# A two-layer graph network: the last projection in float32r passes instead of block sums in fp32

## The chip, the cores and the metric

The kernel runs on one core of one Trainium2 chip. The metric is the device time of one execution in microseconds (us), taken as the median of several runs.

## The reference

Two graph attention layers follow one another on a batch of 64 graphs of 256 nodes with 512 features, each with its own adjacency matrix. Every layer is preceded by a layer norm and a relu, and its result is added to its input. What is computed, cut to what matters:

```python
h = jnp.maximum(_layernorm(x), 0.0)
x = x + L0(adj, h)          # two GAT stages
h = jnp.maximum(_layernorm(x), 0.0)
x = x + L1(h, adj)

# L0: gat(h, W1: 512 -> 4 heads x 256), elu, gat(., W2: 1024 -> 512, one head)
xl = (x @ W).reshape(B, N, H, F)
e = leaky_relu(asrc[:, :, None, :] + adst[:, None, :, :], 0.2)   # asrc, adst: xl times two vectors
attn = softmax(where(mask, e, -1e9), axis=1)
out = einsum('bsdh,bshf->bdhf', attn, xl) + bias

# L1: W_proj: 512 -> 8 heads x 64
xp = einsum('bnd,do->bno', x, W_proj)
scores = leaky_relu(a_src[:, :, :, None] + a_dst[:, :, None, :] + b_att, 0.2)
att = softmax(where(A > 0, scores, -1e30), axis=-1)
out = relu(einsum('bhij,bhjk->bhik', att, xh))
```

All inputs are float32 (the adjacency is int32), and so is the output.

## The kernel before

The work of one graph is a chain of some 80 small steps. Each step is a method of the class `Graph` (one object for each graph). Steps that end in 1 belong to the first GAT stage (four heads), in 2 to the second, in 3 to the last layer (eight heads).

A stage runs like this. `stats` and `norm` make the layer norm of 256 rows (two blocks t = 0, 1 of 128 rows). `away` and `home` write the result to DRAM and read it back in another arrangement, after which `back` turns 128x512 numbers with VectorE's block transpose, so that the features lie across the partitions. `left` makes sums of blocks on GpSimd. The projection follows as a `Product`: the matrix product is cut into 2x2 blocks and done with 7 instead of 8 block products, by the Winograd scheme. Each block product is one of p1 to p7 (TensorE, 128 rows of a chunk against 256 columns and a few logit columns, 2 chunks for a 512-feature input, 4 for 1024 features). The steps q1, q6 and q7 copy running sums to SBUF (tile `kept`, ScalarE, line 61), and q2, q3, c22 and q4 put the four blocks of the result in place (line 261 on VectorE, 259 on ScalarE). The right operand's block sums are made once, at the start (`right`, line 592). `m1a` and `m1b` are the two halves of the first projection, `m2` the second, and `m3` the last one: its weights are `wp_sb`, whose first 8 columns hold the logit vectors folded into W_proj, and `put3` writes the logits to `lg3` and the rest to `xl3`.

Then `exp` makes exponentials of the logits on ScalarE, `ship` and `rows` send them through DRAM to all partitions, `edges` forms the attention weights (one ScalarE and one VectorE instruction for each block, lines 291 and 292), `gat` multiplies them with the projected features (lines 411, 481, 556) and `out` divides by the sum that a column of ones has collected. `again` loads x once more into `x2`, `bias` adds b2 to it (line 370, GpSimd), `out2` adds the second stage, and `store` writes the graph's result. `elu1`, `ez1`, `send2`, `take2` stand between the first and the second stage. `masks`, `caps`, `open`, `cap3` and `edge01` prepare the adjacency.

The order of all steps is written out by hand in three strings: `head` for the start, `order` for one round, and `tail` for the end. A round advances several graphs at once: "-3 m3 q4" is a step of the graph three places behind the newest one. The string `order` runs 61 times, for r = 2 to 62. Each engine executes its own instructions strictly in the sequence of the strings, and a step waits only for its inputs and for a free buffer. All DMAs shown here but a few at the start are issued from SP's queue, in the sequence of the strings too.

Buffers come from pools with a fixed number for each name: `x2` 3, `hs` (the turned input of m1 and m3) 2, `e` 9, `kept` 4, `o` 4, and in PSUM 2 banks of `sum`, 4 of `pm`. The last graph (`gone` false) turns its data on TensorE with identity products (lines 228, 453) and spreads its logits with identity products too (line 254).

After `short_path` a second path for inputs of extreme range stands in the program; it is entered only when the range check asks for it.

## Time and profile before

| | us |
|---|---|
| median of 3 runs | 2969.62 (2968.97 to 2975.85) |
| the profiled execution, its time | 2968.22 |
| its span in the profile | 2966.4 |
| TensorE busy (PE) | 2917.8 |
| VectorE busy (DVE) | 2531.3 |
| ScalarE busy (ACT) | 1711.3 |
| GpSimd busy (POOL) | 1287.4 |

The profile is of one execution. Matrix products overlap in the pipeline, so the mean duration of one is longer than the distance between two starts; the distance is what counts in a full stream. In the groups, a line gives the source line, the engine, the operation, the tile written and the tiles read, the shape and the count, then the busy time in us and the mean duration in ns, and at last the idle time of the engine just before, with what ended it. PEld is the weight load of TensorE, which runs beside PE.

### The profile page before, as it was taken

How to read it: one execution, taken by the hardware profiler on the slowest of the kernel's cores; microseconds unless marked ns; L12 is line 12 of the kernel's file. 1: busy time of each engine (PE TensorE's matmuls, PEld its weight loads, DVE VectorE, ACT ScalarE, POOL GpSimd, SP SyncE). 2: the span in 40 equal slices, each digit the busy share in tenths (PEclk: the TensorE clock that was granted, in tenths of full speed). 3: DMA queues.
4: the chain of work that ended last, by engine and by line, in shares of the span. 5: the costliest groups of instructions: out<-in, count | busy, mean ns of one | idle time of the engine just before them, and what ended most of it. 6: DMA issues, size and time to landing. Idle time of an engine off the chain costs nothing.

```text
span 2966.4 us, 59522 instructions
## 1 busy us (share of the span) xinstructions
PE 2917.8 (98%) x20296; PEld 2531.6 (85%) x20296; DVE 2531.3 (85%) x6370; ACT 1711.3 (58%) x4489; POOL 1287.4 (43%) x1882
## 2 busy tenths in 40 slices
PE   6999999999999999999999999999999999999997
PEld 4888888888888888888888888888888888888886
DVE  8788888888888888888888888888888888888886
ACT  3466565655655655655656556556556556555554
POOL 3443443444444444434444444444444344344433
PEclk9999999999999999999999999999999999999998
DMA  6556555656565665555556565565555556566542
GB/s 193 155 173 180 175 180 171 180 178 179 170 182 176 175 180 174 172 180 177 179 171 185 173 179 173 178 184 167 175 177 174 178 178 179 172 182 176 179 136 73
DMA packets 536859, 513.17 MB, mean 173 GB/s; under 512 B 85736, under 2 KB 373352, under 8 KB 536552
## 3 DMA queue, kind: packets, MB, share of 16 engines
q1 hardware_dynamic: 535176, 507.20, 57.5%
q8 instruction: 165, 2.70, 0.4%
q10 hardware_dynamic: 1376, 2.10, 0.2%
q14 instruction: 142, 1.16, 0.1%
HBM read 332.01 MB, written 168.79 MB: 169 GB/s over the span
## 4 chain that ended last, share of the span: by engine, by line
PE 97%; DVE 1%; DMA 1%; issue 0%; ACT 0%; POOL 0%; SPq 0%; ACTq 0%; DVEq 0%
PE sum L55 38%; PE pm L55 29%; PE pm L411 15%; PE pm L556 8%; PE pm L481 7%; DVE prod L597 0%; DMA w1a_sb<-in_L_gnn_W_dram 0%; DMA xs<-in_x_dram 0%; DMA h<-kept_h 0%; DMA z<-kept_z 0%; DVE e L292 0%; DVE hs L213 0%; ACT h L199 0%; DVE z L419 0%; DMA bc<-kept 0%
## 5 line engine op out<-in xcount | busy, mean ns | idle before, releaser
L291 ACT ACTIVATE wys<-bc,exs_sb 128x256 f32<-128x256 f32 x1646 | 715.4, 468 | 297.4 <-DMA bc<-kept 145.4
L61 ACT ACTIVATE kept<-sum 128x260 f32<-128x260 f32 (+3 forms) x768 | 296.0, 386 | 714.0 <-PE sum L55 713.3
L292 DVE SCALAR_TENSOR_TENSOR e<-wys,exs_sb,cap 128x256 f32<-128x256 f32 x1024 | 444.9, 476 | 62.2 <-ACT wys L291 52.6
L55 PE MATMUL sum<-w_sb,h1s 128*128 128x257 f32 x2048 | 488.1, 380 | 0.6
L411 PE MATMUL pm<-xl,e 128*128 128x257 f32 x2048 | 476.4, 380 | 0.9 <-DVE e L292 0.8
L411 PEld LDWEIGHTS pm<-xl,e 128*128 128x128 f32 x2048 | 387.9, 190 | 60.1 <-DVE e L292 1.7
L55 PEld LDWEIGHTS sum<-w_sb,h1s 128*128 128x128 f32 x2048 | 383.3, 190 | 64.3 <-issue 3.8
L566 POOL TENSOR_TENSOR x<-x,o 128x256 f32<-128x256 f32 x256 | 182.0, 731 | 486.5 <-DVE o L564 484.6
L261 DVE TENSOR_TENSOR xl<-pm,kept 128x256 f32<-128x256 f32 (+2 forms) x768 | 318.1, 415 | 79.1 <-ACT kept L61 40.4
L219 POOL TENSOR_TENSOR hs<-hs 128x256 f32<-128x256 f32 x128 | 109.0, 852 | 617.9 <-DVE hs L213 589.8
L55 PE MATMUL pm<-w_sb,h1s 128*128 128x257 f32 x1536 | 361.6, 384 | 0.0
L55 PEld LDWEIGHTS pm<-w_sb,h1s 128*128 128x128 f32 x1536 | 285.8, 189 | 44.8 <-POOL h1s L219 1.0
L213 DVE STREAM_TRANSPOSE hs<-h 128x512 f32<-128x512 f32 x252 | 283.2, 1150 | 8.4 <-DMA h<-kept_h 8.0
L292 DVE SCALAR_TENSOR_TENSOR e<-wys,exs_sb,mask 128x256 f32<-128x256 f32 x640 | 278.4, 477 | 12.9 <-ACT wys L291 7.0
L449 DVE STREAM_TRANSPOSE h1s<-z 128x512 f32<-128x512 f32 x252 | 260.6, 1104 | 17.6 <-DMA z<-kept_z 17.6
L55 PE MATMUL sum<-w1a_sb,hs 128*128 128x260 f32 x1024 | 269.1, 386 | 4.0 <-DVE w1a_sb L597 3.4
L55 PE MATMUL sum<-wp_sb,hs 128*128 128x264 f32 x1024 | 271.0, 387 | 0.7 <-ACT hs L229 0.7
L55 PE MATMUL sum<-w1b_sb,hs 128*128 128x256 f32 x1024 | 266.4, 383 | 4.9 <-DVE r L417 2.6
L556 PEld LDWEIGHTS pm<-xl,e 128*64 128x64 f32 x8192 | 245.9, 138 | 24.8 <-issue 24.1
L419 DVE SCALAR_TENSOR_TENSOR z<-pm,r,b_sb 128x256 f32<-128x256 f32 x512 | 247.7, 484 | 18.3 <-DVE r L417 0.3
L219 POOL TENSOR_TENSOR h1s<-h1s 128x512 f32<-128x512 f32 x64 | 81.3, 1270 | 412.2 <-DVE h1s L449 405.2
L556 PE MATMUL pm<-xl,e 128*64 128x65 f32 x8192 | 255.8, 223 | 1.9 <-DVE e L292 1.7
(94 smaller groups left out, 4832.0 us busy)
## 6 DMA issues: line engine op xcount, KB each, us to landing
bc<-kept SPq DMA_DIRECT2D x380, 256.0 KB, 4.6
kept_h<-h SPq DMA_DIRECT2D x126, 512.0 KB, 3.5
h<-kept_h SPq DMA_DIRECT2D x126, 512.0 KB, 3.7
kept_z<-z SPq DMA_DIRECT2D x252, 256.0 KB
z<-kept_z SPq DMA_DIRECT2D x252, 256.0 KB, 2.9
xs<-in_x_dram SPq DMA_DIRECT2D x64, 512.0 KB, 6.0
x<-in_x_dram SPq DMA_DIRECT2D x64, 512.0 KB
out_dram<-x SPq DMA_DIRECT2D x64, 512.0 KB
```

The costliest lines, as they stand in the source:

```text
L55: self.nc.tensor.matmul(to[:, :self.n], self.lhs[:, i, c, :], self.rhs[:, i, c, :], start=(first and c == 0), stop=(last and c == self.nk ...
L61: self.nc.scalar.activation(s[:, :self.n], self.sum[:, :self.n], AF.Copy)
L213: nc.vector.transpose(a[:, 4 * t:4 * t + 2].rearrange("p r k (j q) -> p q (r k) j", q=4), h[:, t].rearrange("p (q i c) -> p q c i", q=4, c=4))
L219: nc.gpsimd.tensor_tensor(s1, s3, a22, ALU.add)
L261: nc.vector.tensor_tensor(dst, pm, add, ALU.add)
L291: nc.scalar.activation(wy, bc, AF.Copy, scale=yw)
L292: nc.vector.scalar_tensor_tensor(dst, wy, xw, mask, ALU.max, op)
L411: nc.tensor.matmul(pm[:, :Q + 1], self.e[1, h][:, s, t * P:(t + 1) * P], xl1[:, s, h, L1:], start=(s == 0), stop=(s == T - 1))
L419: nc.vector.scalar_tensor_tensor(self.zt[t][:, sl], pm[:, :Q], r, b1_sb[:, sl], ALU.mult, ALU.add)
L449: nc.vector.transpose(a.rearrange("p k (j q) -> p q k j", q=4), z.rearrange("p (q i c) -> p q c i", q=4, c=4))
L481: nc.tensor.matmul(pm[:, :n], self.e[2][:, s, t * P:(t + 1) * P], xl2[:, s, half, L2:L2 + n], start=(s == 0), stop=(s == T - 1))
L556: nc.tensor.matmul(pv[q:q + 64, h, :], self.e[3, a * G + h][:, s, t * P + q:t * P + q + 64], xl3[:, s, a * G + h, :], start=(s == 0), stop ...
```

## The change

The last projection is no longer a `Product`. Each operand is split into a high and a low part in the type float32r. The weights are split once, at the start: `high` (ScalarE, the raw weights times 1 - 2^-13), `low` (VectorE, the rest), `rest` (VectorE, high minus 2^12 times low) and `lift` (ScalarE, low times 2^12). For each graph and each block of 128 rows, `high3` (ScalarE), `low3` (GpSimd) and `mix3` (VectorE) make three parts of the turned input. For each of the 4 quarters of the result (2 row blocks, 2 column halves) there are three passes of 4 chunks each on TensorE: `u3` (high with high) and `w3` (low with lifted low) into one `sum` bank, and `v3` (mix with rest) into a `pm` bank. `k3` copies the sum times 1 + 2^-12 to SBUF on ScalarE, and `d3` subtracts the v3 result on VectorE and writes it to `xl3`. The two logit columns of each head now lie beside the head's 64 columns, in the weights (`raw3`, `wk_sb`) as in `xl3`, so `lg3` and its adds go.

Buffer numbers change: `x2` 2, `hs` 1 (m1 alone), `e` 7, `kept` 3, `o` 2, `ad` 1, and the norm's small tiles 3; `raw` with 1 and `hk` with 5 buffers are new. The raw projection weights lie in the buffer `h1s` at first.

All three strings are written anew. The diff, with the strings cut to the seam of a round:

```diff
-            self.a1 = work.tile([P, 7, DC // 2, P], F32, name="hs")
+            self.a1 = work.tile([P, 7, DC // 2, P], F32, name="hs", bufs=1)
...
-            self.x2 = work.tile([P, T, D], F32, name="x2", bufs=3)
+            self.x2 = work.tile([P, T, D], F32, name="x2", bufs=2)
...
         def back3(self, t):
-            if self.a3 == 1:
-                self.a3 = work.tile([P, 7, DC // 2, P], F32, name="hs")
-                self.m3 = Product(nc, ps_sum, ps_mm, work, self.a3, wp_sb, put3)
-            (back if self.gone else turn)(self.h, self.a3, t)
-
-        def left3(self):
-            left(self.a3, DC // 2)
+            self.raw = work.tile([P, DC, P], F32, name="raw", bufs=1)
+            (back if self.gone else turn)(self.h, self.raw, t)
+
+        def part(self, i, t):
+            a = self.hk[i, t] = work.tile([P, DC, P], F32R, name="hk", bufs=5)
+            return a
+
+        def high3(self, t):
+            nc.scalar.activation(self.part(0, t), self.raw, AF.Copy, scale=DOWN)
+
+        def low3(self, t):
+            nc.gpsimd.tensor_tensor(self.part(1, t), self.raw, self.hk[0, t].bitcast(F32), ALU.subtract)
+
+        def mix3(self, t):
+            nc.vector.scalar_tensor_tensor(self.part(2, t), self.hk[0, t].bitcast(F32), UP, self.raw, ALU.mult, ALU.subtract)
+
+        def uv(self, pm, i, j, half, t, first, last):
+            for c in range(DC):
+                nc.tensor.matmul(pm[:, :G * (K3 + 2)], self.hk[i, t][:, c], wk_sb[:, j, half, c],
+                                 start=(first and c == 0), stop=(last and c == DC - 1))
+
+        def u3(self, half, t):
+            self.us[half, t] = ps_sum.tile([P, 512], F32, name="sum")
+            self.uv(self.us[half, t], 0, 0, half, t, True, False)
+
+        def w3(self, half, t):
+            self.uv(self.us[half, t], 1, 1, half, t, False, True)
+
+        def k3(self, half, t):
+            s = self.ks[half, t] = work.tile([P, 264], F32, name="kept", bufs=KEPT)
+            nc.scalar.activation(s, self.us.pop((half, t))[:, :264], AF.Copy, scale=UP)
+
+        def v3(self, half, t):
+            self.vs[half, t] = ps_mm.tile([P, 512], F32, name="pm")
+            self.uv(self.vs[half, t], 2, 2, half, t, True, True)
+
+        def d3(self, half, t):
+            def heads(s):
+                return s[:, :G * (K3 + 2)].rearrange("p (h k) -> p h k", h=G)
+            nc.vector.tensor_tensor(xl3[:, t, half * G:(half + 1) * G, :K3 + 2], heads(self.ks.pop((half, t))),
+                                    heads(self.vs.pop((half, t))), ALU.subtract)
...
-        def sums3(self, i):
-            if i == 0:
-                self.sums[3] = right(wp_sb)
-            next(self.sums[3])
...
+        def high(self, half):
+            nc.scalar.activation(wk_sb[:, 0, half], raw3[:, half], AF.Copy, scale=DOWN)
+
+        def low(self, half):
+            nc.vector.tensor_tensor(wk_sb[:, 1, half], raw3[:, half], wk_sb[:, 0, half].bitcast(F32), ALU.subtract)
+
+        def rest(self, half):
+            nc.vector.scalar_tensor_tensor(wk_sb[:, 2, half], wk_sb[:, 1, half].bitcast(F32), -LIFT,
+                                           wk_sb[:, 0, half].bitcast(F32), ALU.mult, ALU.add)
+
+        def lift(self, half):
+            nc.scalar.activation(wk_sb[:, 1, half], wk_sb[:, 1, half].bitcast(F32), AF.Copy, scale=LIFT)
...
     order = """
+        -1 elu1 0 0, -1 ez1 0 1, -3 mix3 1, -2 m2 p3, -3 v3 1 0, -2 m2 q3, -2 m2 p2, -3 d3 1 0, -3 u3 0 0,
+        -3 v3 0 0, -3 w3 0 0, -2 bias 1, -3 low3 1, -1 elu1 1 1, -2 bias 0, 0 away1, 1 load, -3 v3 0 1, 0 home1,
+        -1 elu1 0 1, -2 m2 q2, -2 exp2, -2 ship2, -3 u3 1 1, -3 k3 0 0, 1 stats1 0, -3 w3 1 1, -3 v3 1 1,
+        -3 d3 0 0, -3 u3 0 1, -3 w3 0 1, 0 masks, -3 k3 1 1, 1 stats1 1, -1 send2 0 0, -3 k3 0 1, -1 gat1 2 0,
+        -3 d3 1 1, 0 back1 0, -3 d3 0 1, -1 gat1 3 0, -2 rows2, -1 send2 1 1, 0 back1 1, -1 take2 0 0, -3 batt3,
...
+        -3 edges3 6, 0 m1b p3, -1 m2 p6, -3 out3 0 1, -1 m2 q6, 0 edges1 0, -3 gat3 1 0, -3 gat3 1 1, -1 m2 p7,
+        0 gat1 0 1, -3 out3 1 0, -3 out3 1 1, 0 edges1 3, -3 store, -2 back3 0, 0 gat1 0 0, 0 m1b q3, 0 edges1 1,
+        0 out1 0 0, -1 m2 p5, -2 high3 0, 0 gat1 1 0, -2 low3 0, -2 mix3 0, -2 back3 1, -1 m2 q7, 0 out1 1 0,
+        -1 m2 c22, 0 edges1 2, -1 again, 1 edge01, -2 u3 1 0, 1 norm1 1, 0 gat1 1 1, -2 w3 1 0, 1 norm1 0,
+        -2 k3 1 0, 0 out1 1 1, -1 m2 p4, 0 ez1 0 0, 0 gat1 3 1, 0 gat1 2 1, -2 high3 1, 0 out1 0 1, 0 out1 3 1,
+        0 out1 2 1, 0 ez1 1 1, -1 m2 q4, -3 range
```

## The prediction

> **What bounds the kernel now.** I read the busy table, then the three stages of the span, then TensorE's own waits, then the chain of work that ended last.
>
> ```profile
> PE 2917.8 (98%) x20296; PEld 2531.6 (85%) x20296; DVE 2531.3 (85%) x6370; ACT 1711.3 (58%) x4489; POOL 1287.4 (43%) x1882
> PE 97%; DVE 1%; DMA 1%; issue 0%; ACT 0%; POOL 0%; SPq 0%; ACTq 0%; DVEq 0%
> ```
>
> TensorE is 98% busy and carries 97% of the chain. VectorE, at 85%, is the next engine. By stage (columns: stretch, its length, busy time of PE, PEld, DVE, ACT and POOL, then granted clock, DMA share, GB/s):
>
> ```profile
> 0.00:74.00 74.00, 46.25 (x153) 35.00 (x154) 61.60 (x213) 22.55 (x55) 27.74 (x47) 0.95 0.61 193
> 74.00:148.00 74.00, 70.97 (x324) 60.80 (x324) 58.14 (x133) 36.30 (x96) 30.09 (x41) 1.00 0.53 155
> 148.00:2892.00 2744.00, 2742.97 (x19232) 2387.47 (x19231) 2365.78 (x5897) 1618.07 (x4252) 1204.48 (x1758) 1.00 0.59 176
> 2892.00:2966.00 74.00, 57.56 (x592) 48.30 (x590) 45.75 (x130) 34.36 (x89) 25.05 (x37) 0.90 0.21 74
> ```
>
> A graph is 316 TensorE instructions, so the third row is 19232/316 = 60.9 rounds of 45.1 us, in which TensorE idles 1.03 us in all. The waits of TensorE in that stretch are one line:
>
> ```profile
> PE pm L556 <- issue: 0.2, 1, 0.2
> ```
>
> So in a steady round every TensorE time removed shortens the span, as long as nothing else becomes late. VectorE works 2365.78/2744 = 86% of it, 38.9 us of 45.1.
>
> **What the change removes from TensorE.** The old last projection in the timeline (start, duration, what, count):
>
> ```profile
> 1532.42 1.05 PE L55 MATMUL sum<-wp_sb,hs 128*128 128x264 f32 x4
> 1533.31 1.05 PE L55 MATMUL pm<-wp_sb,hs 128*128 128x264 f32 x4
> 1534.20 1.05 PE L55 MATMUL sum<-wp_sb,hs 128*128 128x264 f32 x4
> ```
>
> Starts are 0.89 us apart for four instructions, 222.5 ns each (the 386 ns of the groups contain overlap). Each fp32 product is two such instructions with two weight loads: the row holds four for two products. Seven pairs of products per graph: 7 x 0.89 = 6.23 us.
>
> **What it adds to TensorE.** Each graph has 4 sums (2 row blocks x 2 column halves) of three passes over 4 chunks: 48 products of 264 columns in float32r. The built program holds one weight load and one matmul for each of these, where fp32 has two. No float32r ran before, so it is bounded. Above: the fp32 instruction of the same 264 columns, 222.5 ns, if the type saves only the second instruction. Below: half of it, 111 ns, if the moving operand too is no longer taken in two parts. A weight load of 128 columns has to hide beside so short a matmul; the nearest rows for that are the identity products of 128 columns in the tail:
>
> ```profile
> 2895.62 1.60 PE L453 MATMUL pm<-ident,z 128*128 128x128 f32 x12
> 2897.06 1.25 PE L55 MATMUL sum<-w_sb,h1s 128*128 128x257 f32 x5
> 2944.61 2.50 PE L254 MATMUL pm<-ident,exs_sb 128*128 128x128 f32 x20 [0.56 <-ACT exs_sb L534]
> ```
>
> Twelve take 1.44 us to the next start, 120 ns each. Twenty last 2.50 us; less the last one's 0.275, that is 2.22/19 = 117 ns. So an instruction with a 128-column load can repeat every 117 to 120 ns, and the load is not added to the matmul. I take 115 ns, between the half (111) and these rows: splitting the weights visibly costs fp32 a second load and stream, and the split of the columns should cost the same again. 48 x 0.115 = 5.52 us. Change per graph: 5.52 - 6.23 = -0.71 us (-0.90 at 111 ns, -0.47 at 120, +4.45 at 222.5). Times 64 graphs: **-45.4 us** (-57.6, -30.1, +284.8).
>
> The Trainium skill bears on both ends. FP8 and Floating Point Precision, section TensorE Precision Notes, counts four passes for true FP32 and names a read truncated to the native width as the reduced form; with that form as one pass, a quarter of 445 ns is 111 ns, by which the sum would be -57.6 us, an estimate. Against the change speaks TensorE: Matmul & The Clock Gate, section Weight-path perf modes: the fast weight load is off for FP32 types. Its section LDWEIGHTS (loading the stationary operand) gives columns/1.2 ns, 107 ns for 128; added to 111 ns that makes 218 ns a product and about +271 us, an estimate, which rows L453 and L254 contradict: they hide such a load.
>
> **The other engines.** From the groups by shape (busy, mean ns):
>
> ```profile
> L428 DVE SCALAR_TENSOR_TENSOR z<-ez,z 128x512 f32<-128x512 f32 x256 | 178.2, 696 | 2.9
> L261 DVE TENSOR_TENSOR xl<-pm,kept 128x256 f32<-128x256 f32 x384 | 158.7, 415 | 5.2 <-PE pm L55 4.7 <-PE pm L556 0.5
> L261 DVE TENSOR_TENSOR xl<-pm,kept 128x260 f32<-128x260 f32 x192 | 81.3, 423 | 69.2 <-ACT kept L61 36.4 <-PE pm L55 32.6
> L261 DVE TENSOR_TENSOR lg<-pm,kept 128x8 f32<-128x8 f32 x192 | 29.5, 154 | 3.5 <-ACT kept L61 2.2 <-PE pm L55 1.2
> L423 ACT ACTIVATE ez<-z 128x512 f32<-128x512 f32 x256 | 158.7, 620 | 7.5 <-DVE z L419 7.5
> L370 POOL TENSOR_TENSOR x<-x,b_sb 128x512 f32<-128x512 f32 x128 | 163.6, 1279 | 31.1 <-DMA x<-in_x_dram 30.8
> ```
>
> VectorE gains four d3 (0.423, the 260-column row) and two mix3 (0.696, the 512-column row), 3.08 us, and loses three adds of 256 and three of 8 columns, 1.71 us: +1.37, so 40.3 us of a 44.4 us round, 91%. ScalarE gains two high3 (0.62) and four k3 (0.39), and loses three copies (0.39) and the two of q4 (0.16 and 0.38): +1.09 on 26.6 us. GpSimd swaps left3's four (0.85 and three of 0.73, 3.05 us) for two low3 (1.28): -0.5 us. That these write float32r is not in any row; I take the float32 price, and no gain: low3 at twice its price would still leave GpSimd under 55%. All of it lies beside TensorE's 44.4 us and costs nothing while each result is on time; if that cover goes, VectorE's next 4 us per round would bound.
>
> **Waits that the new order brings.** The tightest I find goes through the round's seam. x2 has two buffers instead of three, so the reload `again` (on SP's queue, with away1, load and home1 behind it) waits until the store of the graph two before has landed. GpSimd's bias 1 waits for that reload, low3 1 is queued behind bias 1, and w3 1 1 on TensorE waits for low3, with three more float32r groups and two gat1 groups behind it. Price of the chain: a store of 512 KB 3.5 (the row of kept_h), reload 6.0 (the row of xs), bias 1.28, low3 1.28: 12.1 us. Cover: TensorE's work in the new order from the last gat3 plus out3's VectorE and GpSimd parts to w3 1 1, some 14.9 us. Slack 2.8 us. Likewise back3 of the second block waits for low3 of the first (one raw buffer), and six parts share five hk buffers, so that low3 1 waits for u3 0 0 to be done with high3's: both have 1 to 2 us before TensorE asks. The sum tiles alternate between two banks; k3 0 0 follows exp2 on ScalarE, which waits for m2's q2 on VectorE, with about 1 us before u3 0 1. I allow 0.08 us a round, +5 us in 61 rounds (bounds 0 and 0.7). The hs, e, ad, o, kept and small buffers that are trimmed have their last readers half a round before the next writer in the order; nothing.
>
> **Ends.** Head: the four sums of wp (0.81 each, 3.2 us on VectorE) go; low and rest on VectorE come, two each of 1056 columns at about the 1.22 us of the 1028-column sums, 4.9 us, and four ScalarE passes. VectorE is busy 61.6 of the first 74 us, so some of the +1.7 shows: +2 us (-4 to +6, as the whole head is reordered). The tail trades left3 for high3, low3, mix3 in series, about equal: 0 (+-4).
>
> **Sum.** Against the profiled execution (2968.2 us; 1.8 us lies outside its span of 2966.4): 2968.2 - 45.4 + 5 + 2 = 2929.8. The median of the three runs is 1.4 us higher: **2931 us**.
>
> **The rivals.**
> Two-part streams: float32r still takes 222.5 ns. For it: only fp32 was seen. Against: half as many instructions for each product and the column split argued above. 2969.6 + 285 = 3254 us, slower. It decides from 130 ns on, where 48 products cost the old 6.23 us. Chance 0.14.
> The seam or VectorE gives the gain back: waits of 0.4 to 1.2 us per round. For it: 2.8 us slack is less than a landing's own spread (3.5 to 6.0), VectorE at 91%. Against: the order before ran 61 rounds at 86% with 1 us idle. From 2969.6 - 45 + 2 + 24 to +73: 2950 to 3000 us; above 0.7 us a round (43/61) it is slower. Chance 0.20, of which 0.05 faster, 0.07 no change, 0.08 slower.
> Weight load shows at 120 ns: 2946 us, still within the main case.
> Main case, 111 to 120 ns and at most 0.3 us of waits: 2912 to 2948 us, chance 0.64; a remainder of 0.02 goes to slower.
>
> Faster by over 0.3% (9 us, about what a measurement here can tell from no change): 0.64 + 0.05 = 0.69; within 0.07; slower 0.08 + 0.14 + 0.02 = 0.24. The range takes the main case and the seam rival and leaves out two-part streams: 2910 to 3000.
>
> **What would show it.** Right: float32r starts about 115 ns apart, four in 0.46 us; PE busy per round down 0.7 us with idle under 0.2 us; VectorE busy near 91%. Wrong: starts at 220 ns; or TensorE idle of 0.5 us and more per round before L541, released by POOL low3, ACT k3 or VectorE; or in the gat1 and gat3 rows released by VectorE's edges.

## The result, and the profile after

The changed kernel takes 2967.93 us (median of 12 runs, 2965.85 to 2970.23) where the kernel before took 2970.35 us beside it (12 runs, 2967.99 to 2975.85). The ratio is 0.999, 95% interval 0.9981 to 0.9999: no change of a size that counts. The forecast was 2931 us. The profiled execution after took 2966.22 us (span 2964.5), the one before 2968.22 (span 2966.4). So 2.0 us came of the 38 us that the sum had promised.

The busy table and the chain of the kernel after:

```profile
PE 2912.1 (98%) x21576; PEld 2571.5 (87%) x21576; DVE 2602.0 (88%) x6370; ACT 1780.8 (60%) x4557; POOL 1265.4 (43%) x1754
PE 95%; DVE 2%; DMA 2%; ACT 0%; issue 0%; POOL 0%; ACTq 0%; SPq 0%; DVEq 0%
```

TensorE has 1280 instructions more (20 for each of 64 graphs) and is busy only 5.7 us less. It still carries the chain. The same four stretches as before (stretch, length, busy PE, PEld, DVE, ACT, POOL, granted clock, DMA share, GB/s):

```profile
0.00:74.00 74.00, 41.50 (x134) 31.48 (x135) 60.85 (x212) 23.37 (x52) 27.01 (x46) 0.82 0.59 181
74.00:148.00 74.00, 70.52 (x339) 59.81 (x338) 59.54 (x132) 38.89 (x98) 31.40 (x43) 1.00 0.55 161
148.00:2892.00 2744.00, 2743.83 (x20484) 2431.05 (x20483) 2432.76 (x5903) 1682.80 (x4323) 1181.48 (x1633) 1.00 0.58 176
2892.00:2966.00 74.00, 56.20 (x624) 49.13 (x622) 48.88 (x126) 35.73 (x86) 25.53 (x32) 0.89 0.23 73
```

In the third stretch TensorE idles 0.17 us out of 2744. VectorE works 89% of it, 39.9 us of a round (40.3 were forecast). So no wait took the gain: TensorE's own stream is almost as long as it was. Its only wait of 0.15 us or more there is for one copy:

```profile
PE sum L62 <- ACT kept L68: 0.2, 1, 0.2
```

The round (distance between the starts of the same TensorE step in successive rounds, median) was 45.07 us before and is 44.99 us after. The sum had -0.71 us and 0.08 us of waits. Where did 0.6 us go inside a stream that never stops? The timeline of TensorE shows it (start, duration, what, count). First the float32r products:

```profile
1533.04 0.64 PE L541 MATMUL pm<-wk_sb,hk 128*128 128x264 f32 x4
1533.52 0.64 PE L541 MATMUL sum<-wk_sb,hk 128*128 128x264 f32 x4
1534.00 0.64 PE L541 MATMUL pm<-wk_sb,hk 128*128 128x264 f32 x4
```

Groups of four start 0.48 us apart: 120 ns for each product (121 in the mean of all that follow one another), not 115. Then `gat3`, the attention product of the last layer, whose weights have 64 columns. After:

```profile
1507.57 1.02 PE L62 MATMUL pm<-w1b_sb,hs 128*128 128x256 f32 x4
1508.43 1.03 PE L62 MATMUL sum<-w1b_sb,hs 128*128 128x256 f32 x4
1509.39 2.09 PE L593 MATMUL pm<-xl,e 128*64 128x65 f32 x64
1511.41 1.13 PE L62 MATMUL sum<-w1b_sb,hs 128*128 128x256 f32 x4
1512.37 1.03 PE L62 MATMUL pm<-w1b_sb,hs 128*128 128x256 f32 x4
1513.24 1.90 PE L62 MATMUL sum<-w_sb,h1s 128*128 128x257 f32 x8
1515.07 2.09 PE L593 MATMUL pm<-xl,e 128*64 128x65 f32 x64
1517.09 2.01 PE L62 MATMUL sum<-w_sb,h1s 128*128 128x257 f32 x8
1518.93 1.90 PE L414 MATMUL pm<-xl,e 128*128 128x257 f32 x8
1520.66 1.90 PE L62 MATMUL pm<-w_sb,h1s 128*128 128x257 f32 x8
```

and the same product in the trace of before:

```profile
1512.66 1.91 PE L55 MATMUL sum<-w_sb,h1s 128*128 128x257 f32 x8
1514.50 3.95 PE L556 MATMUL pm<-xl,e 128*64 128x65 f32 x128
1518.38 3.75 PE L55 MATMUL pm<-w_sb,h1s 128*128 128x257 f32 x16
1521.96 1.90 PE L55 MATMUL sum<-w_sb,h1s 128*128 128x257 f32 x8
1523.70 4.50 PE L411 MATMUL pm<-xl,e 128*128 128x257 f32 x20
```

Before, its 128 instructions are one block of 3.88 us. The new order puts m1b p4, m1b p3 and m2 p6 into its middle, and makes two blocks of 64 of it, 2.02 us each: 0.15 us more for the same instructions. Around each block the two neighbouring groups are longer too. The four fp32 instructions ahead of the first block take 0.96 us to the next start (1508.43 to 1509.39), where four such instructions away from a block take 0.86 (1507.57 to 1508.43). The four behind it take 0.96 as well. That is 0.1 us on each side, for one block before and two after. Together a second block costs 0.15 + 0.2 = 0.35 us a round.

So, per round: float32r 48 x 0.1208 = 5.80 us for 6.23 us of fp32, -0.43; second block +0.35; sum -0.08, against 45.07 to 44.99 measured. Both prices are read from starts and not from this difference.

### The profile page after: what moved, and what is told of

The parts are those of the page before. It is cut to its first block, busy times and chain, and to the rows that moved or that the text cites. A ratio compares the mean times of both kernels' runs of the same rounds, so it can differ in the third digit from the quotient of the medians.

```text
span 2964.5 us, 61553 instructions
## 1 busy us (share of the span) xinstructions
PE 2912.1 (98%) x21576; PEld 2571.5 (87%) x21576; DVE 2602.0 (88%) x6370; ACT 1780.8 (60%) x4557; POOL 1265.4 (43%) x1754
## 4 chain that ended last, share of the span: by engine, by line
PE 95%; DVE 2%; DMA 2%; ACT 0%; issue 0%; POOL 0%; ACTq 0%; SPq 0%; DVEq 0%
PE sum L62 30%; PE pm L62 22%; PE pm L414 15%; PE pm L593 9%; PE sum L541 8%; PE pm L484 7%; PE pm L541 4%; DMA bc<-kept 1%; DVE e L291 0%; DVE o L634 0%; ACT wys L290 0%; DMA kept<-wt 0%; DMA e<-in_L_gnn_att_dst_dram 0%; DMA w1b_sb<-in_L_gnn_W_dram 0%; DMA batt_sb<-in_L_gnn_b_att_dram 0%; DMA xs<-in_x_dram 0%
## 5 line engine op out<-in xcount | busy, mean ns | idle before, releaser
L414 PE MATMUL pm<-xl,e 128*128 128x257 f32 x2048 | 498.3, 381 | 4.5 <-DVE e L291 3.1
L68 ACT ACTIVATE kept<-sum 128x256 f32<-128x256 f32 (+2 forms) x576 | 218.0, 379 | 324.4 <-PE sum L62 323.9
L533 POOL TENSOR_TENSOR hk<-raw,hk 128x512 fp32r<-128x512 f32 x128 | 165.8, 1295 | 489.9 <-ACT exs_sb L284 277.7
L541 PE MATMUL sum<-wk_sb,hk 128*128 128x264 f32 x2048 | 347.0, 302 | 0.0
L541 PEld LDWEIGHTS sum<-wk_sb,hk 128*128 128x128 f32 x2048 | 287.0, 188 | 11.4 <-ACT hk L530 0.3
L452 DVE STREAM_TRANSPOSE h1s<-z 128x512 f32<-128x512 f32 x252 | 288.1, 1144 | 0.1
L593 PE MATMUL pm<-xl,e 128*64 128x65 f32 x8192 | 271.5, 225 | 5.6 <-DVE e L291 4.8
L373 POOL TENSOR_TENSOR x<-x,b_sb 128x512 f32<-128x512 f32 x128 | 166.5, 1302 | 244.3 <-DMA x<-in_x_dram 127.9
L266 DVE TENSOR_TENSOR xl<-pm,kept 128x256 f32<-128x256 f32 (+2 forms) x576 | 239.0, 415 | 25.3 <-PE pm L62 23.8
L196 POOL TENSOR_SCALAR rstd<-mv 128x2 f32<-128x2 f32 x128 | 28.6, 223 | 514.8 <-DVE mv L192 509.6
```

Of the source, the lines that this page charges most:

```text
L68: self.nc.scalar.activation(s[:, :self.n], self.sum[:, :self.n], AF.Copy)
L266: nc.vector.tensor_tensor(dst, pm, add, ALU.add)
L373: nc.gpsimd.tensor_tensor(self.x2[:, t], self.x2[:, t], b2_sb, ALU.add)
L414: nc.tensor.matmul(pm[:, :Q + 1], self.e[1, h][:, s, t * P:(t + 1) * P], xl1[:, s, h, L1:], start=(s == 0), stop=(s == T - 1))
L452: nc.vector.transpose(a.rearrange("p k (j q) -> p q k j", q=4), z.rearrange("p (q i c) -> p q c i", q=4, c=4))
L541: nc.tensor.matmul(pm[:, :G * (K3 + 2)], self.hk[i, t][:, c], wk_sb[:, j, half, c], start=(first and c == 0), stop=(last and c == DC - 1))
```

## The experiments

Theory A: the stream of TensorE explains all of it, 121 ns per float32r product and 0.35 us for the second block. Rivals: the 120 ns are the weight load's and not the columns'; VectorE at 89% paces the round; something else of the new order costs the 0.35 us. Ratios are to the kernel before, run beside each. Below, "four" or "eight" counts TensorE instructions; an fp32 product is two of them, a float32r product one.

**The block split in the kernel before.** Two edits of the string `order` of before; the first moves m2 p7 into the middle of gat3, the second m2 p2:

```diff
-        -1 m2 p7, -2 home3, -3 edges3 6, -3 gat3 0 0, -3 edges3 5, -3 gat3 1 0, ..., -3 gat3 1 1,
-        -1 m2 q7, ..., -3 gat3 0 1, 0 edges1 0, -1 m2 p2,
+ e1     -3 gat3 0 0, -3 gat3 0 1, -1 m2 p7, ..., -3 gat3 1 0, ..., -3 gat3 1 1, -1 m2 q7, ..., -1 m2 p2,
+ e5     -1 m2 p7, ..., -3 gat3 0 0, ..., -3 gat3 1 0, ..., -1 m2 p2, -3 gat3 1 1, -1 m2 q7, ..., -3 gat3 0 1,
```

> The kernel before, with one change in the string of a round: the four gat3 steps, which ran as one block of 128 TensorE instructions, are two blocks of 64 with m2 p7 between them, as the changed kernel has them. Theory A (a change between 128-column and 64-column weights costs TensorE about 0.1 us each way, and the new order pays it twice as often): a round of 45.07 us becomes 45.3 to 45.4 us, 61 rounds give +15 to +21 us, about 2987 us. Rival B (the two blocks cost nothing of themselves, the lost time of the changed kernel lies in VectorE or in waits at the round's seam): within 3 us of before.

> The kernel before with its gat3 block cut in two another way: m2 p2, which came right after the block, is moved into its middle, behind gat3 1 0 and out3 0 0. The first such cut cost 1.22 us a round, of which 0.8 us was a wait of m2 p2 for a product's bank that out3 frees; this one should not make that wait. Theory A (a second block costs 0.35 us a round: 0.09 before it, 0.10 after it, 0.15 within): 45.07 becomes 45.4 us, +21 us, about 2991 us, with TensorE idle under 0.1 us a round. Rival B (only waits cost, the cut is free): 2966 to 2973 us, or slower only by the idle time that the waits list.

Measured: 3038.76 us for 2970.08 (1.0232, 1.0218 to 1.0246) and 3050.78 for 2968.88 (1.0276, 1.0259 to 1.0293); rounds of 46.29 and 46.47 us. The timeline of the first:

```profile
1501.52 2.09 PE L556 MATMUL pm<-xl,e 128*64 128x65 f32 x64
1503.53 2.01 PE L55 MATMUL sum<-w_sb,h1s 128*128 128x257 f32 x8
1505.47 2.09 PE L556 MATMUL pm<-xl,e 128*64 128x65 f32 x64
1508.39 3.71 PE L55 MATMUL pm<-w_sb,h1s 128*128 128x257 f32 x16 [0.84 <-DVE r L562]
```

The first block takes 2.01 us (1501.52 to 1503.53), as in the kernel after, and the eight between the blocks take 1.94 us instead of 1.74: the 0.35 us, without any float32r. But the rounds grew by 1.22 and 1.40. The rest is a wait of 0.84 us behind the second block, where TensorE wants a PSUM bank that out3 on VectorE has not given back yet; by the starts it costs 0.90 us (1505.47 to 1508.39 is 2.92 us, not 2.02). The second order was meant to avoid this wait and has it in the middle of its second block, which takes 3.07 us instead of 2.02 by the starts. The expected price is there in the stream, and the expected time is not, for want of a cover; with the stop added, 45.07 + 0.35 + 0.90 = 46.32 and 45.07 + 0.35 + 1.05 = 46.47 are the rounds that were measured.

**The price of one float32r product.** Streams of products with nothing between them behind the last graph, 40 for each width:

```diff
+    def probe(n, lhs, rhs, count, rows=P):
+        pm = ps_mm.tile([P, 512], F32, name="pm")
+        for i in range(count):
+            nc.tensor.matmul(pm[:rows, :n], lhs(i), rhs(n), start=True, stop=True)
...
+    for n in (256, 264):
+        probe(n, lambda i: one, lambda n: wide[:, :n], 40)
+    for n in (128, 264):
+        probe(n, lambda i: a[:, i % DC, :64], lambda n: wide[:, :n], 40, 64)
```

> The changed kernel, with streams of matmuls added behind the last graph, where TensorE has nothing else to do: float32r with a 128-column weight and 64 to 512 moving columns, the same with the weight's columns read from one address, with a 64-column weight, fp32 beside them, and runs of 64-column products between 128-column ones. Theory A (the 120 ns of a float32r product are the weight load's): the start-to-start time is flat at 120 ns from 64 to about 280 columns and grows from there by 0.42 ns a column (512: 216 ns); with a 64-column weight 128 moving columns take 60 to 70 ns; with the weight from one address 264 columns fall to about 112 ns. Rival B (the moving stream of four-byte columns is the bound, 0.455 ns a column): 128 columns take 60 to 117 ns, 512 take 233 ns, and 264 columns stay at 120 ns whatever the weight. The whole run is some 25 us longer than the changed kernel.

Measured: one execution of 3096.77 us, of which the distances between starts in the tail count (medians of 40): 112 ns for 64 columns (113 for 192 where the granted clock was full again; the 128 ran at half of it, 213 ns, and fp32 instructions of 128 columns take 112), 120 for 256 and 264, 131 for 288, 147 for 320, 180 for 400, 227 for 512. From 264 columns on that is 0.44 to 0.46 ns a column; up to 192, 112 ns is a floor. The floor is the load of 128 weight columns: with weights of 64 columns, 128 columns take 60 ns, and 264 still 120. So the 264 columns of this kernel are bound by their columns, 264 x 0.455 = 120 ns, and not by the load; weights of one address give the same 120. The fp32 instruction of 264 columns takes 222.5 ns in the same tail, and a product needs two of them: a float32r product is 3.7 times cheaper, not the 3.87 times that 115 ns would give.

In the last part of the tail blocks of 32 and 64 instructions with 64-column weights (L862) stand between eight fp32 instructions (L859), with no other engine at work (VectorE, ScalarE and GpSimd have 0.3 us in the 135 us of the tail):

```profile
3044.60 1.15 PE L862 MATMUL pm<-w_sb,ident 128*64 128x65 f32 x32
3045.68 2.00 PE L859 MATMUL pm<-w_sb,ident 128*128 128x257 f32 x8
3047.61 1.15 PE L862 MATMUL pm<-w_sb,ident 128*64 128x65 f32 x32
...
3056.65 2.09 PE L862 MATMUL pm<-w_sb,ident 128*64 128x65 f32 x64
3058.67 2.00 PE L859 MATMUL pm<-w_sb,ident 128*128 128x257 f32 x8
...
3070.51 17.60 PE L864 MATMUL pm<-w_sb,ident 128*128 128x257 f32 x80
```

By the starts, 32 take 1.08 us and 64 take 2.02, and the eight between two blocks 1.93, where the last line has 1.74 for eight. The price of a block is there without any other engine. It is not the width of the weights alone that costs: in the same tail two float32r streams, of 128 and then of 64 weight columns, follow each other in a step of 115 ns, and the step from 64 to the 128 of the next stream, of fp32 instructions, is 120 ns, as within a stream. The instructions of the blocks are also fp32, have 65 columns, and come in pairs that start 7 ns apart, one for each half of the output's rows. Which of this sets the price was not tried.

**Less on TensorE.** The products of w3 (low with low) are left out, 16 of 48 (u3 then closes the sum itself):

```diff
         def w3(self, half, t):
-            self.uv(self.us[half, t], 1, 1, half, t, False, True)
+            pass
```

> The changed kernel without the 16 w3 products of a graph (the low parts are still made, but not multiplied, so the result lacks their share): 16 x 0.1208 = 1.93 us less TensorE work a round, all else the same. Theory A (a round is TensorE's work and nothing else, VectorE's 39.9 us still hide): -118 to -124 us, 2844 to 2850 us, less than 0.2 us of TensorE idle a round. Rival B (VectorE, at 88.7% of the round, already holds the round): it gives back half or more, 2900 us and above, with TensorE idle released by VectorE.

Measured: 2893.73 us (0.9745, 0.9731 to 0.976); the round falls by 1.22 us of the 1.93 taken out. The waits of TensorE and the busy times (order as above) from 300 to 2700 us:

```profile
PE sum L62 <- DVE hs L219: 23.3, 55, 0.5
300.00:2700.00 2400.00, 2373.95 (x17429) 2072.27 (x17428) 2224.33 (x5306) 1520.97 (x3881) 1087.59 (x1475) 1.00 0.60 182
```

Now TensorE waits 0.4 us a round for VectorE, which is busy 92.7%. Both theories hold in part: TensorE's work sets the round of the kernel after, and when the round is some 1.2 us shorter, VectorE's results come late.

**The block joined in the kernel after.** gat3's four parts stand together again, in eight orders. The core of the first (behind m2 p6):

```diff
-        -2 norm3 0, -3 edges3 5, -3 gat3 0 1, 0 m1b q7, -3 gat3 0 0, -2 away3, 0 m1b c22, -3 edges3 7,
...
-        -3 edges3 6, 0 m1b p3, -1 m2 p6, -3 out3 0 1, -1 m2 q6, 0 edges1 0, -3 gat3 1 0, -3 gat3 1 1, -1 m2 p7,
+        -2 norm3 0, -3 edges3 5, 0 m1b q7, -2 away3, 0 m1b c22, -3 edges3 7,
...
+        -1 m2 p6, -1 m2 q6, -3 gat3 0 1, -3 gat3 0 0, -3 out3 0 0, 0 edges1 0,
+        -3 out3 0 1, -3 gat3 1 0, -3 gat3 1 1, -1 m2 p7,
```

> The changed kernel, with the two gat3 blocks of a round moved together (after m2 p6), out3 and m1b q3 moved with them. Theory A: the round falls from 44.98 to 44.65 us, 61 rounds give -15 to -21 us, about 2948 us; a wait of TensorE for left2 or for edges3 in the new place could take part of it back. Rival B: no change, 2965 to 2971 us.

Measured: 3019.87 us (1.0168, 1.0155 to 1.0182), round 45.88. The block takes 3.88 us again, but the work that stood behind its first half (m1b p4, p3 and m2 p6) is asked for 2 us earlier, and its copies and sums are not ready:

```profile
PE sum L62 <- ACT kept L68: 24.6, 52, 0.5
PE sum L62 <- POOL h1s L225: 13.0, 52, 0.3
```

The next five put m2 p6 behind gat3 and move m1b's steps, c22 and back2 to make the copies early:

```diff
+ e6   -2 away3, 0 m1b c22, 0 m1b p4, ..., -3 gat3 0 1, -1 back2 1 0, -1 left2, -3 gat3 0 0, 0 edges1 0, ..., -3 gat3 1 1, -1 m2 p6,
+ e7   as e6, but back2 1 0 and left2 behind gat3 0 0 and edges1 0
+ e8   as e6, but back2 1 0 and left2 behind edges3 7
+ e9   as e6, but m1b p5 in front of m2 p1, and c22 in front of back2 1 1 and norm3
+ e10  as e9, but back2 1 1 in front of c22
```

> The changed kernel with one block of gat3 per round, as tried before, but with other work placed over the two copies that TensorE waited for: m1b p7 ahead of m2 p1, m2 p6 behind the block, gat1 0 1 between m2 p6 and p7; VectorE's edges3 4 and 6 ahead of back2 1 0. Theory A: 0.35 us a round less than the changed kernel if no wait takes it, 44.65 us a round and about 2946 us; each 0.1 us of new waits in a round gives 6 us back. Rival B (joining brings nothing in itself): 2965 us or more with no TensorE idle time.

> As the run before, but edges1 0 stands ahead of back2 1 0 on VectorE, so gat1 0 1 has its weights earlier and left2 starts 0.9 us later. Theory A: about 2946 us; if m2 p6 then waits for left2, some 0.1 to 0.9 us a round come back (2952 to 3000 us), shown as idle released by GpSimd. Rival B: 2965 us or more with no TensorE idle time.

> As the first of these, but back2 1 0 stays ahead of edges3 4 as in the changed kernel, so left2 starts early and edges3 4 and 6 come 1.1 us later. Theory A: about 2946 us; if gat3 1 0 then waits for edges3 6, some 0.1 to 0.9 us a round come back, shown as idle released by VectorE's edges. Rival B: 2965 us or more with no TensorE idle time.

> The joined block once more, from the first of the last three, whose round lost 1.04 us because m1b p3 waited for c22 on VectorE: now m1b p5 stands ahead of m2 p1, and c22 ahead of back2 1 1. Theory A (a second gat3 block costs 0.35 us a round, and nothing else keeps TensorE): the round falls from 45.76 to 44.65-44.75 us, about 2945 to 2952 us, 5 to 8 tenths of a per cent under both kernels. Rival B (joining brings nothing): 2965 us or more with no TensorE idle time; with new waits, 6 us for each 0.1 us of them in a round.

> The same with c22 behind back2 1 1, so VectorE is held by c22's wait for q7 later. Theory A: 2945 to 2952 us, as the run before within 0.1 us a round, whichever of the two has no wait. Rival B: 2965 us or more with no TensorE idle time.

The waits are those from 300 to 2700 us, the longest per round. The list counts only stops of 0.15 us and more between the recorded ends, so a stop can cost more by the starts:

| order | time, us | ratio (95%) | round, us | first wait of TensorE |
|---|---|---|---|---|
| e6 | 3022.82 | 1.0185 (1.0168 to 1.0202) | 45.76 | 0.8, m1b p3 for c22 |
| e7 | 3083.03 | 1.0388 (1.0371 to 1.0406) | 46.76 | 0.8, the same, and up to 2.1 for out3 |
| e8 | 3027.37 | 1.0199 (1.0182 to 1.0216) | 45.90 | 0.8, the same |
| e9 | 3015.39 | 1.0153 (1.0139 to 1.0167) | 45.67 | 0.4, gat3 for its edges |
| e10 | 3012.51 | 1.0147 (1.0132 to 1.0163) | 45.66 | 0.2, gat3 for its edges |

All are slower than the kernel after. In each, waits that the split order covers come back, and are worth more than the split costs: 1.0 us a round or more, by the rounds against 44.64. Two more put m2 p6 in front of gat3 again, with GpSimd's sums earlier:

```diff
+ e11  ..., 0 m1b c22, -1 back2 1 0, -1 left2, -2 norm3 1, -2 norm3 0, -3 edges3 5, ..., -1 m2 p6, -1 m2 q6, -3 gat3 0 1,
+ e12  ..., 0 m1b c22, -2 norm3 1, -2 norm3 0, -3 edges3 5, -1 back2 1 0, -1 left2, ..., -1 m2 p6, -1 m2 q6, -3 gat3 0 1,
```

> The kernel after with the last projection's attention product (gat3, 128 instructions of 64-column weights) in one block, after m2 p6, and m2 p6 late enough that q7, q6 and c22 of m1b come first; the steps back2 1 0 and left2 stand right behind c22, ahead of edges3 5. Theory A (the second block costs 0.35 us a round, and only the lateness of copies took it back in the earlier joined orders): if left2, c22 and the edges are on time, a round of 44.65 us and about 2946 us; each 0.1 us of wait per round gives 6 us of that back. Rival B (some other cost of the new order, not the second block, makes the round 44.99): 44.95 us or more with no idle TensorE, 2965 us or more. Rival C (VectorE's work cannot be put in any order that leaves the block whole): a wait of 0.3 us or more a round on VectorE or GpSimd, 2965 us or more with idle TensorE.

> As the run with left2 right behind c22, but back2 1 0 and left2 stand behind norm3 and edges3 5 on VectorE. Theory A: if left2 is on time for m2 p6, 44.65 us a round and about 2946 us; edges3 comes 1.3 us earlier than in the other order and left2 later by as much, so the wait, if there is one, is for GpSimd's sums (m2 p6) rather than for the edges. Rival B: 44.95 us or more with no idle TensorE. Rival C: a wait of 0.3 us or more a round on one of the two, 2965 us or more.

Measured: 3329.1 us (1.1211, 1.1196 to 1.1227) and 3199.9 us (1.0764, 1.0749 to 1.0779), rounds of 51.2 and 49.4: the third rival's waits, but 6.2 and 4.4 us a round more than after, far beyond the 0.3 us that it named as the least. The timeline of the first, and two stretches of the same round with the granted clock behind the five busy times:

```profile
1492.08 3.77 PE L62 MATMUL sum<-w_sb,h1s 128*128 128x257 f32 x8 [3.88 <-ACT kept L68]
1495.78 4.50 PE L593 MATMUL pm<-xl,e 128*64 128x65 f32 x128
1490.00:1496.00 6.00, 3.92 (x12) 2.74 (x14) 1.73 (x4) 2.60 (x8) 1.89 (x2) 0.51 0.50 153
1496.00:1500.00 4.00, 4.00 (x126) 4.00 (x126) 2.14 (x7) 1.75 (x5) 0.00 (x0) 0.88 0.01 4
```

m2 p6 waits 3.9 us, by the release in the trace for q1's copy, with GpSimd's sums for it ending at the same time. gat3 is queued behind it, and behind gat3's buffers stand the edges that VectorE must write next (its waits for gat3 are 361.6 us in this run). And TensorE's granted clock is down to 0.51 and 0.88 in the stretches with the wait and behind it, and there eight instructions take 3.7 us (1492.08 to 1495.78) instead of 1.74, and the block 4.4 us instead of 3.88. The waits therefore cost more than they last. In the second order m2 p6 waits up to 2.6 us for GpSimd's sums, as its expectation named (101.3 us from 300 to 2700 us), and the granted clock is 0.97.

**VectorE relieved.** mix3 is left out (the pass v3 reads the high part), once in the order of after and once in that of e10:

```diff
         def mix3(self, t):
-            nc.vector.scalar_tensor_tensor(self.part(2, t), self.hk[0, t].bitcast(F32), UP, self.raw, ALU.mult, ALU.subtract)
+            self.hk[2, t] = self.hk[0, t]
```

> The kernel after without VectorE's mix3 (0.85 us, two a round; the v3 pass reads the high part instead, so its result lacks the correction by the low part). Theory A: TensorE's stream, with its two blocks of 64-column weights, sets the round, so 1.7 us less on VectorE changes nothing: 44.99 us a round, 2966 us (2962 to 2970). Rival C (VectorE at 88 to 93% paces the round): up to 0.5 us less a round, 2940 to 2960 us. It is the control for the joined order without mix3.

> The same without mix3, in the joined order whose only wait was for VectorE's edges3 (m2 p6 behind gat3): gat3 stands in one block of 128. Theory A: with 1.7 us less in front of the edges on VectorE the waits of 0.7 us are gone, and what is left is one block of 64-column weights instead of two: 44.65 us a round, 0.35 us less than the control, some 21 us, 2945 us (2940 to 2952). Rival B (the second block is not what the new order costs): 44.95 us and 2965 us with no idle TensorE. Rival C: a wait for the edges of 0.3 us or more stays.

Measured: 2965.16 us (0.9986, 0.9977 to 0.9995), round 44.99; and 3013.69 (1.0155, 1.0141 to 1.0169), round 45.67. The first settles a rival: 1.7 us less on VectorE leaves the round as it was, so VectorE does not pace the kernel after. The second is a miss: the joined order has the round it had with mix3, so mix3's share of VectorE's load is not what delays it either. Its timeline shows three stops:

```profile
1484.91 1.02 PE L62 MATMUL sum<-w1b_sb,hs 128*128 128x256 f32 x4
1486.03 1.13 PE L62 MATMUL pm<-w1b_sb,hs 128*128 128x256 f32 x4
1487.09 2.55 PE L593 MATMUL pm<-xl,e 128*64 128x65 f32 x80
1489.82 1.90 PE L593 MATMUL pm<-xl,e 128*64 128x65 f32 x48 [0.18 <-DVE e L291]
1491.65 2.01 PE L62 MATMUL sum<-w_sb,h1s 128*128 128x257 f32 x8
1493.84 1.10 PE L414 MATMUL pm<-xl,e 128*128 128x257 f32 x4 [0.18 <-DVE r L599]
```

The block lasts 4.56 us (1487.09 to 1491.65) instead of 3.88: at its 81st instruction it wants edges3 6, the last edge before it. Ahead of it the two groups of four take 1.12 and 1.06 us instead of 0.86 and 0.96, since m1b p3 starts late (in e6 and e8 the list has it waiting for c22). Both stops come in every round: by the medians 0.68 and 0.34 us. The third, the eight behind the block with 2.19 us to the next start instead of 1.84, where gat1 wants a bank that out3 has not given back, is of this round; the median is 1.85. So the sum closes: 44.99 - 0.35 + 0.68 + 0.34 = 45.66 us, against 45.67 measured. The one block does save 0.35 us, and two stops cost 1.02.

**mix3 moved off VectorE**, the whole sum kept:

```diff
+            nc.scalar.activation(self.part(2, t), self.hk[0, t].bitcast(F32), AF.Copy, scale=1.0 / LIFT)
...
+            nc.gpsimd.tensor_tensor(self.hk[2, t], self.hk[2, t].bitcast(F32), self.hk[1, t].bitcast(F32), ALU.subtract)
...
-            nc.vector.scalar_tensor_tensor(self.part(2, t), self.hk[0, t].bitcast(F32), UP, self.raw, ALU.mult, ALU.subtract)
```

> The kernel after with mix3 taken off VectorE: ScalarE writes 2^-12 times the high part (0.62 us), GpSimd subtracts the low part from it (1.28 us), and low3 1 stands ahead of bias 1, v3 0 1 behind w3 1 1. The whole sum is computed. Theory A: 44.99 us a round as before, 2966 us (2962 to 2972), if GpSimd's chain of low3 and mix3 is on time; each 0.1 us of wait in the seam costs 6 us. Rival: GpSimd's chain shows before v3, 0.3 us or more a round, 2985 us or more.

> The same move of mix3, with gat3 joined in one block as in the run without mix3. Theory A: 44.65 us a round and 2945 us (2940 to 2955), faster than both kernels by 0.8%, if neither the edges nor GpSimd's chain is late. Rival B: 2965 us with no idle TensorE. Rival C: waits of 0.3 us or more a round for the edges or for low3 and mix3 on GpSimd, 2965 to 3000 us.

Measured: 3040.71 us (1.0243, 1.0229 to 1.0257), round 46.20; and 3087.08 (1.04, 1.0385 to 1.0414), round 46.86. The rival came in: v3 waits for GpSimd's chain in every round (300 to 2700 us of the first of the two); by the starts the whole 1.2 us of the first is lost between the float32r passes.

```profile
PE pm L543 <- POOL hk L535: 31.5, 52, 0.6
```

**The two stops taken away.** From e10's order; cap3, norm3, m1b q4 and m2 q1 go behind edges' exponentials, the edges change places, and out3 0 1 goes in front of edges1 0:

```diff
+        -3 edges3 5, -3 edges3 6, -2 norm3 1, -2 norm3 0, -2 away3, 0 rows1, 0 m1b p4, -3 edges3 4, 0 m1b p3, -3 edges3 7,
+        0 m1b q4, -1 m2 q1, 0 m1b q3, -2 home3, -3 gat3 0 1, -1 back2 1 0, -1 left2, -3 gat3 0 0, 0 cap3,
+        -3 out3 0 1, 0 edges1 0, -3 gat3 1 0, -3 out3 0 0, -3 gat3 1 1, -1 m2 p6, -1 m2 q6, 0 gat1 0 1,
```

> The kernel after, whole, with gat3 in one block and what made the earlier joined orders wait taken away on ScalarE and in the buffers rather than on VectorE: cap3, norm3, m1b q4 and m2 q1 stand behind the exponentials of edges3 that they preceded, edges3 0 comes before edges3 1 (its buffer is the first that gat3 gives back) and edges3 7 last, and out3 0 1 stands ahead of edges1 0. Theory A: if the waits of 0.7 us inside the block and 0.35 us behind it go, a round of 44.65 us and 2946 us (2943 to 2955); each 0.1 us of wait left costs 6 us. Rival B (the second block is not what the new order costs): 44.95 us or more with no idle TensorE, 2965 us. Rival C: the waits only move (back3 for the later norm3, gat1 for its edges), 0.3 us a round or more, 2965 us or more.

The expectation takes the 0.35 us behind the block for a stop of every round, which it is not. Measured: 3135.47 us (1.0552, 1.0536 to 1.0569), round 47.55. Rival C: the waits moved (300 to 2700 us).

```profile
PE pm L414 <- DVE e L291: 47.3, 50, 2.7
PE pm L593 <- DVE e L291: 24.0, 50, 0.5
```

The edges are later, not earlier: VectorE waits 224.7 us for ScalarE's exponentials between 300 and 2700 us (84.2 us in the same stretch of the kernel after), now behind the moved norm3.

**A third block.** One pair exchanged in the kernel after, nothing asked for earlier:

```diff
-        -3 gat3 1 0, -3 gat3 1 1, -1 m2 p7,
+        -3 gat3 1 0, -1 m2 p7, -3 gat3 1 1,
```

> The kernel after with one pair of steps exchanged: m2 p7 stands between gat3 1 0 and gat3 1 1, so that the 64-column weights come in three blocks (64, 32, 32) instead of two. Nothing on TensorE comes earlier than in the kernel after, so nothing should have to wait. Theory A (each further block costs 0.15 us inside and 0.1 us in each neighbour): 0.35 us a round more with no idle TensorE, 45.34 us, 21 us more over 61 rounds, 2987 us (2983 to 2993). Rival B (a change of the weight's width costs nothing by itself, the second block's cost came from elsewhere): 44.99 us and 2966 us.

Measured: 3010.98 us (1.0143, 1.0127 to 1.016), round 45.72, 0.73 us more than after. Its timeline:

```profile
1537.93 1.15 PE L593 MATMUL pm<-xl,e 128*64 128x65 f32 x32
1539.01 2.01 PE L62 MATMUL sum<-w_sb,h1s 128*128 128x257 f32 x8
1540.95 1.15 PE L593 MATMUL pm<-xl,e 128*64 128x65 f32 x32
1542.03 2.00 PE L414 MATMUL pm<-xl,e 128*128 128x257 f32 x8
1543.87 1.90 PE L62 MATMUL pm<-w_sb,h1s 128*128 128x257 f32 x8
```

From the first of these starts to the last it is 5.94 us; the same instructions take 5.59 in the kernel after (1515.07 to 1520.66: block 2.02, eight 1.84, eight 1.73). That is the 0.35 us of the forecast. The other 0.4 us is in a later gat1 part, whose eight take 2.12 us in the median instead of 1.73; its products wait for a bank that VectorE gives back later, since out3 1 1 comes later there, as far as the trace tells. 44.99 + 0.35 + 0.39 = 45.73 us, against 45.72.

What is shown and what stays open: the price of a block is read as 0.35 us from the starts in four kernels (after, e1, e18 and the tail of e3), and in four (e1, e5, e14, e18) the price and the stops together give the measured round within 0.03 us. No run shows the price by itself as time: each order that joined or split the block also moved a wait of 0.4 us or more. No kernel with the whole computation beat the kernel after, why each joined order is late is settled only as far as the trace names the wait, and what in a block makes its price is open.

## Why the prediction was wrong

**What bounds the kernel, and that every TensorE time removed counts: right.** e4 returned 1.22 of 1.93 us, with VectorE's cover ending there; e13 shows that VectorE is not the bound.

**What is removed, 6.23 us a graph: right.** The tail of e3 has 222.5 ns for the fp32 instruction as well.

**What is added, 48 x 0.115: mis-sized.** It is 0.1208. The prediction saw the right bounds (111 to 120) and chose 115, reasoning that half an fp32 instruction is a float32r product. The runs show 0.455 ns a column at 264 columns against 222.5/264/2 = 0.421 for each half of the fp32 instruction. The rows taken as the bound of the weight load gave the right number for another reason: the load's floor is 112 ns, and the columns make the 120. 48 x 0.0058 = 0.28 us a round. The estimate of 111 ns that was worked out from the Trainium skill, FP8 and Floating Point Precision, section TensorE Precision Notes, is 9 ns too low here.

**What is moved: the step that failed.** The prediction looked at the new order for waits alone, and priced moved TensorE steps at nothing, since the same instructions stay. It did not ask what stands beside what. The new order has m1b p4, m1b p3 and m2 p6 between the parts of gat3, where before they were one block, and the trace of before already showed the price of a block's border: 1.84 us for the eight in front of it (1512.66 to 1514.50), 1.74 elsewhere (1521.96 to 1523.70). The second block is 0.35 us a round, half of the 0.71 us that was to be gained.

**Waits of the seam, +5 us: none came.** The third stretch has 0.2 us of TensorE waits: -0.08 us a round. (The 3.5 to 6.0 us that the prediction calls a landing's spread are the medians of two different transfers, the store of kept_h and the load of xs.) The rival of the seam gave the right time (2950 to 3000) by the wrong mechanism: it asked for 0.4 to 1.2 us of idle TensorE per round. That the measured time lies between the forecast's bounds is luck: the bounds took it in for that rival's sake.

**Other engines: right in sum.** VectorE is at 89% where 91% was expected. mix3 was priced 0.696 us and takes 0.848:

```profile
L537 DVE SCALAR_TENSOR_TENSOR hk<-hk,raw 128x512 fp32r<-128x512 f32 x128 | 108.5, 848 | 1.8 <-ACT hk L530 1.5
```

**Head and tail, +2 us: +5.5.** The second graph's gat2 starts at 146.56 us instead of 140.29, 6.3 us later, and what follows the 61st graph's gat2 is 0.8 us shorter. Most is in the first stretch, 41.50 us busy on TensorE instead of 46.25, at a clock of 0.82 instead of 0.95; which step of the new head delays it was not tried.

Together, in the 59 rounds between these starts: forecast 59 x (-0.71 + 0.08) = -37 us, measured -7.4 (2656.34 us for 2663.74). The product's price makes 16 us of this miss of 30, the second block 21, the waits that did not come -5, and -3 comes of something that nobody forecast: some rounds of before are longer than the median (up to 45.96 us, 45.15 in the mean), those of after hardly (45.02); why was not looked into. The head and the tail make the other 7 us (+5.5 instead of about -1 with the five graphs outside these rounds). 30 + 7 = 37, against 36.4 (-38.4 expected, -2.0 found in the profiled executions).

## What to carry to other kernels

When an order is rewritten, compare not only which instructions each engine has but what stands beside what in its queue: a border between kinds of work can have a price, and here the trace of before showed it in the neighbours of the block that was there. Where an engine is full, price a new kind of instruction by its floor and by its columns separately, and take the upper of the two where the gain hangs on it: 5.8 ns times 3072 products was 40% of the gain expected here. And an order that looks wasteful may be the cover of a wait: here 0.35 us for a second block spared 1.0 us and more of waits for copies, edges and banks in each of the joined orders that were tried.

## What the runs showed of the hardware

- A stream of float32r products with 128 weight columns (e3) starts one every 112 ns at 64 columns and 113 at 192, every 120 ns at 256 and 264, and takes 0.44 to 0.46 ns a column from 264 to 512 (227 ns); with 64 weight columns and 128 columns, one every 60 ns.
- A block of fp32 instructions with 64 weight columns and 65 columns costs 0.1 us in each neighbour of 128 weight columns, and 0.15 us inside: 32 instructions take 1.08 us, 64 take 2.02, 128 take 3.88. Where one stream of e3 follows another, the change of the weight's width alone costs nothing that shows (115 ns from 128 to 64 columns, 120 ns back).
- With a wait of 3.9 us a round in the middle of the kernel TensorE's granted clock was lower (0.51 and 0.88 in the stretches shown, 0.94 over the steady part of e11), and a stream of 40 products of 64 columns in e3 was followed by a stretch with half of the clock, though TensorE was busy:

```profile
2960.00:2971.00 11.00, 11.00 (x56) 11.00 (x56) 0.00 (x0) 0.00 (x0) 0.00 (x0) 0.52 0.01 2
```

  The kernel after, without that stream, has a granted clock of 0.50 from 2960.1 us on too, with TensorE done, so the stream need not be the cause. What sets this off was not tried.
- VectorE's scalar_tensor_tensor of 128x512 takes 848 ns on the average for mix3 (758 in the median, 0.68 to 1.80 us for single ones), and 684 ns for the same shape at line 431.
